# One unit's input product moves from GpSimd to VectorE in two thirds of the jobs of a selective-scan layer

## The chip, the cores and the metric

The kernel runs on one core of a Trainium2 chip. The metric is device time in microseconds of that core, as the median of three timed runs. One further execution was taken with the hardware profiler; its page and its trace are what the document reads. The engines are named as the profile names them: PE (TensorE matmuls; PEld its weight loads), DVE (VectorE), ACT (ScalarE), POOL (GpSimd), SP (the queue that issues the DMAs).

## The reference

An image batch (8, 192, 56, 56) goes through four residual layers, each `x = x + layer(groupnorm(x))`. Layer 0 is an involution. Layers 1, 2 and 3 are selective state-space blocks (Mamba), and this change touches layer 1 alone. Cut to what matters there:

```
# layer 1: 192 channels are cut into 3 slices of 64, each slice is one sequence of 3136 tokens
xs = layernorm(x) cut into 3 slices
xz = xs @ in_proj_W.T                     # 512 channels xi, 512 channels z
xc = silu(causal conv of xi, 4 taps)
dbl = xc @ x_proj_W.T                     # 4 columns for dt, 16 for B, 16 for C
dt = softplus(dbl[:4] @ dt_proj_W.T + b)
h  = h * exp(dt * A) + (dt * xc) * B      # 512 channels x 16 states, step by step along the sequence
y  = sum over states of h * C + xc * D
out = (y * silu(z)) @ out_proj_W.T
```

## The kernel before

Layer 1 walks over 8 images x 7 chunks of 448 tokens x 3 slices: 168 jobs. The three slices of a chunk are three jobs in a row, in slot 0, 1 and 2 (`jobs[i][0]`); "second- and third-slot jobs" are those of slots 1 and 2. After a chunk's third job, the layer norm and the projection of that chunk run inside the next slot-0 job.

A job has 512 channels x 16 states. They are cut into 16 units m = 0..15: 4 groups j of 128 channels, and in each group 4 quarters q of 4 states. A unit's tile `uhg` has 128 partitions (32 channels x 4 states) and 4 rows of 448 tokens, in 9 rotating buffers. For every unit:

- **product** `uhg = rep * B`: (dt x) times B. For some units VectorE makes it (`inputs_by_vector`, L754), from B in the one PSUM bank `b`, which PE fills with a selection matmul (`spread_b`, L723). For the others GpSimd makes it (`inputs_by_pool`, L748), from B in rows that a DMA has spread in SBUF (`row_in`). Here `pool_units` holds the odd units: eight each.
- **decays** (`decays`, L729): ACT writes exp(dt A) to the PSUM tiles `da0` and `da1`, one for each half of the unit.
- **scan** (L758): VectorE, two instructions, one for each half, on `uhg` in place; it needs `da` and the product.
- **keep** (L762): ACT copies the last column for the next chunk; `inputs_begin` (L737) copies it into the first column of a later unit's tile.
- **readout** (L767): GpSimd multiplies by C in place.
- **reduce** (L776): PE adds over the states into the bank `y`, behind a first matmul with D (L773). `gated` (L792): VectorE multiplies a finished group into the gate `zs`.

The order on each engine is that in which the loop over units issues (the scheduler is manual). In unit k it is: row DMAs, gated, reduce(k-3), planned steps, scan(k, first half), decays(k+1, first half), product of unit k+2 on GpSimd if it is one of its units, readout(k-2), product of unit k+1 on VectorE, `spread_b(k+2)`, planned steps, scan(k, second half), keep(k), decays(k+1, second half).

The planned steps are the next job's projections, put into 32 places (two for each unit) by `places`, with the stretches of `bounds`. For layer 1 the silu block has the places 6 and 7, that is unit 3. There ACT loads another function table (L596), makes silu on `xc` of the next job (1792 columns) and on the gates `zs` of the running job (L577), and loads the first table again (L569). Beside it, behind `spread_b` in unit 3, PE has the output projection of the job before (`out_proj`, L1054 and L1056), whose result ACT copies in unit 4 (L1061). In unit 4 PE has `xproj` (L601) and then `spread_b` for unit 6. Softplus has units 7 and 8 for a next job in slot 1, and units 9 and 10 otherwise.

`nothing` (L782) issues matmuls with zeros, so that PE has work in places where little is planned. Layers 2 and 3 have three channel groups (`nd == 3`), 12 units a job and another set of GpSimd units.

Of the kernel before, what the change touches and what calls it, by code (L numbers as in the profile page):

```python
# [86 lines left out]
def conv_mamba_stack(ctx: ExitStack, tc: tile.TileContext, a, out):  # L87
# [483 lines left out]
    def with_gates(ops, u):  # L571


        def all_ops():
            ops()
            if u is not None:
                nc.scalar.activation(u.zs, u.zs, AF.Silu)  # L577

        table_block(all_ops)
# [112 lines left out]
    def ssm_layer(pool, w, jobs, n_slots):  # L692


        nd = w.nd
        units = [(i, j, q) for i in range(len(jobs)) for j in range(nd) for q in range(NQ)]
        groups = [(i, j) for i in range(len(jobs)) for j in range(nd)]
        per_job = nd * NQ
        pool_units = {1, 3, 5, 7, 9, 11, 13, 15} if nd == 4 else {1, 3, 6, 7, 9, 11}
        pool_rows = sorted({m % NQ for m in pool_units})  # L700
        us = [Layer() for _ in jobs]
        carry = []
        for s in range(n_slots):
# [13 lines left out]
        def spread_b(k):  # L717

            if k in by_pool:
                return  # L720
            i, j, q = units[k]
            brow[k] = banks.b.tile([128, 512], F32, tag="b", name="b")
            nc.tensor.matmul(brow[k][:, :T], lhsT=pick_b[:, q, :], rhs=us[i].parts, start=True, stop=True)  # L723

        def decays(k, h):
            i, j, q = units[k]
            t = banks.da[h]
            for r in range(2):
                nc.scalar.activation(  # L729
                    t[:, 64 + 449 * r : 512 + 449 * r], reps[k // NQ][:, 2 * h + r, 0, :], AF.Exp, scale=w.neg_a[:, j * NR + 2 * h + r, q : q + 1]  # L730
                )

        def inputs_begin(k):
            i, j, q = units[k]
            uhg[k] = pool.tile([128, NR, T + 1], F32, tag="uhg", name="uhg", bufs=9)
            before = zeros[:, :NR] if jobs[i][1] else carry[jobs[i][0]][:, j, q, :]
            nc.scalar.copy(uhg[k][:, :, 0:1], before.unsqueeze(2))  # L737

        by_pool = {k for k in range(len(units)) if (k % per_job) in pool_units}

        def inputs_by_pool(k):
            if k not in by_pool:
                return
            i, j, q = units[k]
            b = us[i].rows[0, q].unsqueeze(1).to_broadcast([128, NR, T])
            nc.gpsimd.tensor_mul(uhg[k][:, :, 1:], reps[k // NQ][:, :, 1, :], b)  # L748

        def inputs_by_vector(k):  # L750
            if k in by_pool:
                return
            b = brow[k][:, :T].unsqueeze(1).to_broadcast([128, NR, T])
            nc.vector.tensor_mul(uhg[k][:, :, 1:], reps[k // NQ][:, :, 1, :], b)  # L754

        def scan(k, h):
            v = uhg[k][:, 2 * h : 2 * h + 2, :].rearrange("p r t -> p (r t)")
            nc.vector.tensor_tensor_scan(v, banks.da[h][:, 63:961], v, 0.0, ALU.mult, ALU.add)  # L758

        def keep(k):  # L760
            i, j, q = units[k]
            nc.scalar.copy(carry[jobs[i][0]][:, j, q, :].unsqueeze(2), uhg[k][:, :, T:])  # L762

        def readout(k):
            i, j, q = units[k]
            v = uhg[k][:, :, 1:]
            nc.gpsimd.tensor_mul(v, v, us[i].rows[1, q].unsqueeze(1).to_broadcast([128, NR, T]))  # L767

        def reduce(k):
            i, j, q = units[k]  # L770
            if q == 0:
                ys[k // NQ] = banks.y.tile([128, 512], F32, tag="y", name="y")
                nc.tensor.matmul(ys[k // NQ][:, :T], lhsT=w.dd[:, j, :], rhs=us[i].xc[:, j, :], start=True, stop=False)  # L773
            y = ys[k // NQ]
            for r in range(NR):
                nc.tensor.matmul(y[32 * r : 32 * r + 32, :T], lhsT=fold, rhs=uhg[k][:, r, 1:], start=False, stop=(q == NQ - 1))  # L776

        def nothing(k, n):

            if k >= 0 and units[k][2] < NQ - 1:  # L780
                for _ in range(n):
                    nc.tensor.matmul(  # L782
                        ys[k // NQ][:, : nd * 112], lhsT=zeros, rhs=w.dd.rearrange("p j e -> p (j e)")[:, : nd * 112],
                        start=False, stop=False,
                    )

        def load_of(steps):
            return sum(st.cost for st in steps if st.matmuls)

        def gated(g):  # L790
            i, j = groups[g]
            nc.vector.tensor_mul(us[i].zs[:, j, :], us[i].zs[:, j, :], ys[g][:, :T])  # L792

        n_places = 2 * per_job
        def bounds(job):

            silu = 8 if nd == 3 else 6
            softplus = silu + (6 if nd == 3 else 8 if job[0] == 1 else 12)
            return (0, silu), (silu, silu + 2), (silu + 2, softplus), (softplus, softplus + 1), (softplus + 2, softplus + 4), (softplus + 4, n_places)

        def places(*stretches):

            plan = [[] for _ in range(n_places)]
            for steps, first, end in stretches:
                todo, debt = list(steps), 0.0
                for p in range(first, end):
                    room, closed = (sum(st.cost for st in todo) + debt) / (end - p) - debt, False
                    while todo and (room > 1e-6 and not closed or p == end - 1):  # L810
                        if (todo[0].block if p % 2 else todo[0].settles) and p < end - 1:
                            break
                        plan[p].append(todo[0])
                        closed = todo[0].closes
                        room -= todo.pop(0).cost
                    debt = max(0.0, -room)
            return plan
# [12 lines left out]
        for k in range(3):  # L830
            inputs_begin(k)
        inputs_by_vector(0)
        spread_b(1)
        inputs_by_pool(0)
# [6 lines left out]
        def load_when_free(k):  # L841

            g = len(reps)
            if g < len(groups) and k >= NQ * g - NQ - 1 and groups[g][1] in us[groups[g][0]].ops:
                load_ops(g)

        for k, (i, j, q) in enumerate(units):
            m = k % per_job
            if m == 0:

                fetch, outs, rest = tail
                if i + 1 < len(jobs):
                    u = us[i + 1]
                    at = bounds(jobs[i + 1])
                    stretches = *jobs[i + 1][2](u, us[i], outs), rest + jobs[i + 1][3](u)
                    plan = places(*((steps, *p) for steps, p in zip(stretches, at)))
                else:
                    gates = Step(None, lambda: with_gates(lambda: None, us[i]), 0, 0.3, block=True)
                    plan = places(([gates], 4, 6), (outs + rest, 8, n_places))
                plan[3][:0] = [Step(None, fetch, 2, 0.0)]  # L860

            if i + 1 < len(jobs) and m - (per_job - NQ) in pool_rows:
                us[i + 1].row_in(0, m - (per_job - NQ))
            if i and m < NQ:
                us[i].row_in(1, m)
            if k >= NQ + 3 and q == 3:
                gated(k // NQ - 1)
            if k >= 3:
                reduce(k - 3)

            more = 3 - math.ceil(load_of(plan[2 * m] + plan[2 * m + 1]))
            nothing(k - 3, more > 2)
            bg.run(plan[2 * m])
            nothing(k - 3, more > 0)
            load_when_free(k)
            scan(k, 0)
            if k + 1 < n_units:
                decays(k + 1, 0)
            if k + 3 < n_units:
                inputs_begin(k + 3)  # L880
            if k + 2 < n_units:
                inputs_by_pool(k + 2)
            if k >= 2:
                readout(k - 2)
            if k + 1 < n_units:
                inputs_by_vector(k + 1)
            if k + 2 < n_units:
                spread_b(k + 2)
            bg.run(plan[2 * m + 1])
            nothing(k - 3, more > 1)  # L890
            load_when_free(k)
            scan(k, 1)
            keep(k)
            if k + 1 < n_units:
                decays(k + 1, 1)
            if m == per_job - 1:
                tail = jobs[i][4](us[i])
# [333 lines left out]
```

## Time and profile before

| | |
|---|---|
| median of the runs | 25021.5 us (25021.35 to 25040.56) |
| the profiled execution | 25031.88 us, its span 25030.1 us |
| layer 1, first scan of its first job to that of layer 2 | 1683 to 17177 us, 15494 us |
| busy share of the span | PE 85%, DVE 90%, ACT 68%, POOL 93% |
| POOL busy in the three jobs from 7170.86 to 7445.08 us | 270.06 of 274.22 us |
| DVE busy in the same stretch | 251.96 us |
| one product on POOL (L748) and on DVE (L754) | 3990 ns, 1997 ns |
| one half scan (L758), one readout (L767) | 2008 ns, 3678 ns |
| mean granted TensorE clock | 0.82 |

How to read it: a row of groups gives the line in the kernel, the engine, the operation, what is written from what, the shape, how often, then the busy time in us and the mean of one in ns, then the idle time of the engine just before it and what ended that. PEclk is the TensorE clock that was granted, as a share of full speed; in this trace it is either whole or half at any moment, and it changes on a fixed grid of 3.41 us.

### The profile page before, as it was taken

To read this page: it belongs to the slowest core of one execution; us is meant where nothing else is said; L and a number is where in the kernel's file an instruction comes from. 1 tells how busy PE (TensorE), PEld (TensorE's weight loads), DVE (VectorE), ACT (ScalarE), POOL (GpSimd) and SP (SyncE) were. 2 spreads that over 40 slices of the span, in tenths; PEclk is the share of its full clock that TensorE was granted. 3 is DMA by queue.
4 is the path that set the end of the run, shared out by engine and by line. 5 is a ranking of instruction groups with operands and counts; after the bars stand their busy time and mean duration, and the time that the engine had idled before them with its cause. 6 is when DMAs were issued, how large, how long until landed. Compare 5 with 4: busy or idle time off the path is not lost.

```text
span 25030.1 us, 232222 instructions
## 1 busy us (share of the span) xinstructions
PE 21294.5 (85%) x71980; PEld 6723.5 (27%) x71980; DVE 22624.9 (90%) x15661; ACT 16939.4 (68%) x32354; POOL 23378.2 (93%) x6772
## 2 busy tenths in 40 slices
PE   9988888888888888888888888888888887888888
PEld 3322222222222222222222222222333332333332
DVE  8879999999999999999999999997999998999998
ACT  1137777777777777777777777776777776777777
POOL 4459999999999999999999999998999998999999
PEclk9987777777777777777777777778888888888888
DMA  4433333333333333333333333333434443444443
GB/s 108 102 103 125 121 120 125 123 122 121 126 122 122 123 123 121 124 121 122 125 123 121 124 120 123 126 121 112 137 132 137 139 139 123 138 140 143 139 143 127
DMA packets 1184873, 3132.62 MB, mean 125 GB/s; under 512 B 163756, under 2 KB 446404, under 8 KB 1183496
## 3 DMA queue, kind: packets, MB, share of 16 engines
q1 hardware_dynamic: 1180824, 3116.70, 37.9%
q8 instruction: 565, 9.26, 0.1%
q14 instruction: 684, 5.60, 0.1%
q10 hardware_dynamic: 2800, 1.06, 0.0%
HBM read 2399.92 MB, written 555.55 MB: 118 GB/s over the span
## 4 chain that ended last, share of the span: by engine, by line
DVE 33%; PE 27%; ACT 17%; issue 11%; POOL 6%; DMA 5%; SPq 1%; DVEq 0%; POOLq 0%; ACTq 0%
DVE uhg L758 24%; ACT da L729 8%; DVE uhg L754 6%; PE y L776 4%; PE mm L635 4%; POOL uhg L767 4%; PE mm L416 3%; DMA rows<-bc 2%; PE y L782 2%; POOL uhg L748 2%; ACT L569 2%; PE y L773 2%; DMA rep<-ops 2%; PE y_inv L451 2%; PE mm L612 2%
## 5 line engine op out<-in xcount | busy, mean ns | idle before, releaser
L758 DVE TENSOR_TENSOR_SCAN uhg<-da,uhg 128x898 f32<-128x898 f32 x8064 | 15905.2, 2008 | 1283.9 <-ACT da L729 1272.0
L767 POOL TENSOR_TENSOR uhg<-uhg,rows 128x1792 f32<-128x1792 f32 x4032 | 14744.6, 3678 | 262.0 <-ACT carry L762 254.5
L729 ACT ACTIVATE da<-rep,k 128x448 f32<-128x448 f32 x16128 | 10253.6, 636 | 1659.5 <-DVE uhg L758 1280.4
L748 POOL TENSOR_TENSOR uhg<-rep,rows 128x1792 f32<-128x1792 f32 x2016 | 8043.7, 3990 | 489.8 <-DMA rows<-bc 235.6
L776 PE MATMUL y<-uhg,k 128*32 128x448 f32 x32256 | 4799.6, 671 | 738.5 <-POOL uhg L767 736.5
L754 DVE TENSOR_TENSOR uhg<-rep,b 128x1792 f32<-128x1792 f32 x2016 | 4025.6, 1997 | 444.5 <-PE b L723 399.9
L762 ACT COPY carry<-uhg 128x4 f32<-128x4 f32 x4032 | 787.3, 195 | 3545.3 <-DVE uhg L758 3452.2
L773 PE MATMUL y<-xc,w_d 128*128 128x448 f32 x2016 | 1505.0, 841 | 1437.3 <-DVE zs L792 1435.8
L782 PE MATMUL y<-w_d,k 128*128 128x448 f32 (+1 forms) x5276 | 2492.0, 580 | 0.0
L776 PEld LDWEIGHTS y<-uhg,k 128*32 128x32 f32 x32256 | 696.5, 117 | 3845.4 <-issue 2186.1
L635 PE MATMUL mm<-dbl,w_dt 36*128 36x448 f32 (+1 forms) x2016 | 1488.5, 851 | 150.1 <-ACT k L617 150.1
L1082 PE MATMUL mm<-v,w_in 96*128 96x448 f32 x2688 | 1460.9, 676 | 160.4 <-ACT zs L674 69.6
L782 PEld LDWEIGHTS y<-w_d,k 128*128 128x128 f32 x5276 | 1048.0, 213 | 1473.8 <-issue 1446.2
L1026 PE MATMUL mm<-xs,k 128*128 128x448 f32 x2688 | 1211.5, 585 | 120.6 <-ACT zs L674 108.7
L436 POOL TENSOR_TENSOR x<-x,one 96x448 f32<-96x448 f32 x560 | 633.3, 1135 | 669.1 <-DVE one L428 651.5
L428 DVE TENSOR_TENSOR prod<-mm,shifted 128x448 f32<-128x448 f32 x1680 | 932.4, 609 | 207.9 <-PE mm L416 187.5
L1109 PE MATMUL mm<-xin,w_conv 128*128 128x448 f32 x2688 | 1076.4, 543 | 1.9 <-ACT xin L674 1.0
L612 PE MATMUL mm<-dbl,k 16*16 16x448 f32 x1120 | 684.3, 699 | 424.7 <-ACT dbl L605 424.7
L773 PEld LDWEIGHTS y<-xc,w_d 128*128 128x128 f32 x2016 | 450.2, 262 | 2098.0 <-DVE zs L792 1419.4
L647 PE MATMUL mm<-xc,k 128*128 128x448 f32 x2016 | 972.2, 593 | 32.8 <-DVE dt L650 31.7
L1044 PE MATMUL mm<-xs,k 64*128 64x448 f32 x1344 | 860.6, 749 | 98.3 <-ACT zs L674 98.3
L723 PE MATMUL b<-k,k 96*128 96x448 bf16 x2016 | 826.5, 410 | 129.7 <-DVE uhg L754 129.5
(134 smaller groups left out, 19622.5 us busy)
## 6 DMA issues: line engine op xcount, KB each, us to landing
rep<-ops SPq DMA_DIRECT2D x4032, 448.0 KB, 5.8
ops<-dt SPq DMA_DIRECT2D x1008, 448.0 KB, 3.2
rows<-bc SPq DMA_DIRECT2D x1792, 224.0 KB, 6.2
shifted<-xpad SPq DMA_DIRECT2D x672, 179.0 KB, 4.6
xg<-stream SPq DMA_DIRECT2D x168, 336.0 KB, 3.9
xr<-stream SPq DMA_DIRECT2D x168, 336.0 KB, 5.2
stream<-xr SPq DMA_DIRECT2D x112, 336.0 KB, 3.3
xs<-xg SPq DMA_DIRECT2D x224, 112.0 KB, 2.3
```

The lines of the kernel that those rows point to most:

```text
L612: nc.tensor.matmul(u.left[m][:NS, :T], lhsT=ident[:NS, :NS], rhs=u.dbl[:NS, :], start=True, stop=False)
L635: nc.tensor.matmul(u.dps[j][:, :T], lhsT=w.dtw[:, j * 128 : (j + 1) * 128], rhs=u.dbl[:nk, :], start=True, stop=True)
L729: nc.scalar.activation(t[:, 64 + 449 * r : 512 + 449 * r], reps[k // NQ][:, 2 * h + r, 0, :], AF.Exp, scale=w.neg_a[:, j * NR + 2 * h + r, ...
L748: nc.gpsimd.tensor_mul(uhg[k][:, :, 1:], reps[k // NQ][:, :, 1, :], b)
L754: nc.vector.tensor_mul(uhg[k][:, :, 1:], reps[k // NQ][:, :, 1, :], b)
L758: nc.vector.tensor_tensor_scan(v, banks.da[h][:, 63:961], v, 0.0, ALU.mult, ALU.add)
L767: nc.gpsimd.tensor_mul(v, v, us[i].rows[1, q].unsqueeze(1).to_broadcast([128, NR, T]))
L773: nc.tensor.matmul(ys[k // NQ][:, :T], lhsT=w.dd[:, j, :], rhs=us[i].xc[:, j, :], start=True, stop=False)
L776: nc.tensor.matmul(y[32 * r : 32 * r + 32, :T], lhsT=fold, rhs=uhg[k][:, r, 1:], start=False, stop=(q == NQ - 1))
L782: nc.tensor.matmul(ys[k // NQ][:, : nd * 112], lhsT=zeros, rhs=w.dd.rearrange("p j e -> p (j e)")[:, : nd * 112], start=False, stop=False,)
L1026: nc.tensor.matmul(pm[:, :T], lhsT=w.inconv[:, k, j * 128 : (j + 1) * 128], rhs=ck.xs[:, i, 2 - 2 * k : 2 - 2 * k + T], start=(k == 0), st ...
L1082: nc.tensor.matmul(pm[:, :T], lhsT=w.inw[:, k, m * 128 : (m + 1) * 128], rhs=ck.v[:, k, :], start=(k == 0), stop=(k == NCT - 1),)
```

## The change

In layer 1, in jobs of slot 1 and 2 (the last job of the layer excepted), unit 5 is taken out of the set of GpSimd. Its product is then VectorE's, and it isn't issued where VectorE's products stand (in the middle of the unit before): it is issued at the end of unit 3, behind the second half scan. `at[1][0]` is 6 for layer 1, so `at[1][0] // 2` is 3. `multiplied` keeps the product from being issued twice. `spread_b(5)`, which did nothing while unit 5 was GpSimd's, now puts a matmul into PE's queue in unit 3. That is 111 jobs: 111 POOL instructions less, 111 DVE instructions and 111 matmuls (each with a weight load) more. The rows of B that GpSimd reads are still loaded (`pool_rows` names the same quarters). For layers 2 and 3 the expression gives unit 6, which is GpSimd's, so nothing changes there.

```
-        pool_units = {1, 3, 5, 7, 9, 11, 13, 15} if nd == 4 else {1, 3, 6, 7, 9, 11}
-        pool_rows = sorted({m % NQ for m in pool_units})
+        def pool_units(i):
+            if nd == 3:
+                return {1, 3, 6, 7, 9, 11}
+            return {1, 3, 5, 7, 9, 11, 13, 15} - ({5} if jobs[i][0] and i + 1 < len(jobs) else set())
+        pool_rows = (1, 2, 3) if nd == 3 else (1, 3)
...
-        by_pool = {k for k in range(len(units)) if (k % per_job) in pool_units}
+        by_pool = {i * per_job + m for i in range(len(jobs)) for m in pool_units(i)}
+        multiplied = set()
...
         def inputs_by_vector(k):
-            if k in by_pool:
+            if k in by_pool or k in multiplied:
                 return
+            multiplied.add(k)
             b = brow[k][:, :T].unsqueeze(1).to_broadcast([128, NR, T])
             nc.vector.tensor_mul(uhg[k][:, :, 1:], reps[k // NQ][:, :, 1, :], b)
...
             scan(k, 1)
+            if i + 1 < len(jobs) and m == at[1][0] // 2 and k + 2 not in by_pool:
+                inputs_by_vector(k + 2)
             keep(k)
```

## The prediction

> **What bounds the kernel now.** First the page: busy time, the chain, the groups.
>
> ```profile
> PE 21294.5 (85%) x71980; PEld 6723.5 (27%) x71980; DVE 22624.9 (90%) x15661; ACT 16939.4 (68%) x32354; POOL 23378.2 (93%) x6772
> ...
> DVE 33%; PE 27%; ACT 17%; issue 11%; POOL 6%; DMA 5%; SPq 1%; DVEq 0%; POOLq 0%; ACTq 0%
> ...
> L748 POOL TENSOR_TENSOR uhg<-rep,rows 128x1792 f32<-128x1792 f32 x2016 | 8043.7, 3990 | 489.8 <-DMA rows<-bc 235.6
> ...
> L754 DVE TENSOR_TENSOR uhg<-rep,b 128x1792 f32<-128x1792 f32 x2016 | 4025.6, 1997 | 444.5 <-PE b L723 399.9
> ```
>
> POOL is the busiest engine and is 6% of the chain that ended last; DVE, PE and ACT are 77% of it. So the second view is who waited for whom, cut to layer 1 (1683 to 17177 us):
>
> ```profile
> DVE uhg L758 <- ACT da L729: 731.9, 407, 3.8
> ...
> DVE uhg L754 <- PE b L723: 341.1, 221, 2.7
> ...
> POOL uhg L767 <- ACT carry L762: 199.7, 171, 4.0
> ...
> PE y L776 <- POOL uhg L767: 169.9, 143, 3.8
> ```
>
> DVE waits for ACT's decays (the two table blocks of a job) and for PE's spread of B. POOL waits 171 times for a unit that isn't scanned yet. Those waits lie in units 10 to 14 of slot 1 and at the end of slot 0: there POOL has caught up with VectorE, once in every three jobs, so it carries no debt along. A test of this in the trace: in slot-0 jobs without an image's end, the readout of unit 0 starts 5.2 to 6.7 us behind its scan, by chance of the job, and the job takes 94.15 to 94.22 us whatever that lag is. Only one with 7.3 us is longer, 94.44. So POOL, 98% busy in layer 1, runs behind a pace that VectorE, ACT and PE set.
>
> Third, the timeline of one slot-1 job around its unit 3, PE's and VectorE's rows:
>
> ```profile
> 7279.11 1.02 PE L773 MATMUL y<-xc,w_d 128*128 128x448 f32 x2 [3.10 <-DVE zs L792]
> 7280.06 1.70 PE L776 MATMUL y<-uhg,k 128*32 128x448 f32 x8
> 7281.69 1.75 PE L1054 MATMUL mm<-xs,k 64*64 64x448 f32 x2
> 7283.37 4.99 PE L1056 MATMUL mm<-zs,w_out 128*64 128x448 f32 x8
> 7288.29 0.96 PE L776 MATMUL y<-uhg,k 128*32 128x448 f32 x8
> 7289.18 3.20 PE L601 MATMUL mm<-xc,w_x 128*36 128x448 f32 x8
> 7292.31 0.36 PE L723 MATMUL b<-k,k 96*128 96x448 bf16 x1
> ...
> 7280.92 1.99 DVE L754 TENSOR_TENSOR uhg<-rep,b 128x1792 f32<-128x1792 f32 x1
> 7282.83 2.01 DVE L758 TENSOR_TENSOR_SCAN uhg<-da,uhg 128x898 f32<-128x898 f32 x1
> 7287.69 5.87 DVE L758 TENSOR_TENSOR_SCAN uhg<-da,uhg 128x898 f32<-128x898 f32 x3 [2.85 <-ACT da L729]
> 7293.47 2.00 DVE L754 TENSOR_TENSOR uhg<-rep,b 128x1792 f32<-128x1792 f32 x1
> ```
>
> VectorE's hole of 2.85 us is the silu block. The last DVE row is unit 6's product; its L723 ended at 7292.67, 0.80 us before. PE has no hole from 7279.11 on, and runs at half clock in 7280.1 to 7287.0 (the stretches in which PE's clock is half are in the trace; here two steps of its 3.41 us grid), since it stood still for 3.10 us before. The same place in a job that kept the full clock:
>
> ```profile
> 7100.26 3.22 PE L1056 MATMUL mm<-zs,w_out 128*64 128x448 f32 x8
> ...
> 7107.43 0.36 PE L723 MATMUL b<-k,k 96*128 96x448 bf16 x1
> ```
>
> Its L723 ends at 7107.79, 4.1 us before unit 6's product. Read in this way, 67 of 108 jobs of slots 1 and 2 have 0.8 us there, 7 have 2.5, 34 about 4.
>
> Last, the grid. Units 8 and 9 run up to and hold the softplus in slots 1 and 2. They take 13.74, 14.85 and 11.56 us in three jobs with the same instructions, by where the half-clock stretches fall:
>
> ```profile
> 7125.86:7139.60 13.74, 13.74 (x45) 4.39 (x43) 10.87 (x9) 12.02 (x21) 13.74 (x4) 0.73 0.15 58
> 7307.46:7322.31 14.85, 14.85 (x44) 4.83 (x42) 10.87 (x9) 12.03 (x21) 14.85 (x5) 0.66 0.15 60
> 7588.54:7600.10 11.56, 11.56 (x43) 4.17 (x43) 10.95 (x8) 11.10 (x19) 11.56 (x4) 0.85 0.19 74
> ```
>
> (The first column is the stretch, the third from the right the granted clock.) Three jobs in a row take 275.33 and 274.22 us in turn, together 549.55, which is 161 steps of 3.4133 us: the loop has locked to the clock's grid.
>
> **The change part by part.**
>
> POOL loses 111 products of 3.99 us, 443 us. I take 0 of it as gain: its cover isn't needed, POOL waits already. Ends: 0, and 443 us if every one of those waits were POOL's debt in disguise (a rival). What it does: POOL's lag falls by up to 4 us in slots 1 and 2 and in the slot 0 behind them; in slot 1 it becomes waiting for scans.
>
> VectorE gains 111 products of 1.997 us, 222 us. Each starts behind the second half scan of unit 3 (7284.84) and ends at about 7286.8; the decays come at 7287.65. The silu block on ACT (table load, two silus, table load, 7280.46 to 7286.33 in its timeline) hides it with 0.85 us to spare, so 0. If B were late, that spare would go first. What it needs is B in the bank: L723 for unit 5 must follow unit 4's product (one bank, ends 7282.91), 0.06 us for the semaphore and 0.37 at half clock, so it is ready at 7283.4, 1.4 us early. Behind the new product on VectorE's queue stands only the scan of unit 4. ACT's keep and decays wait for the scan before it. Buffers are free: unit 5's tile is the one that POOL would have written some 10 us before.
>
> PE gains 111 matmuls of 0.36 us, and here is the cost, by order and not by length: L723 for unit 5 stands in PE's queue behind the reduce and ahead of L1054, and it waits for VectorE. L1054 started at 7281.69; now it starts at 7283.4, 1.7 us later. PE idles 1.2 us, and the whole queue (L1054, L1056, reduce, L601, L723 of unit 6) moves. How far depends on the clock:
>
> - The half clock ends at the same step of the grid, 7287.0. Then fewer of the eight L1056 rows (0.75 us each at half, 0.375 at full) are slow: the end of L1056 moves by 0.9 to 1.05 us, L723 of unit 6 by as much; 0.80 us of that is spare, so VectorE loses 0.1 to 0.3 us.
> - It lasts one step more, 3.41 us. All of L1054 and L1056 is slow, 7.7 us: they end at 7291.1 where 7288.3 was, L1061 on ACT and the decays of unit 5 come 1.3 us late, L723 of unit 6 2.6 us: VectorE loses 1.8 us.
>
> Which: in the trace, half clock ends behind a step in which matmuls with 96 or 128 contraction rows filled 0.65 to 0.73 or more; those with 16, 36 or 64 (L1054) hardly count. With the new wait L1056 fills 0.55 of the second step in slot 1 (the step ends 8.0 us behind the unit's first scan) and 0.66 in slot 2 (8.3 us). So I take 1.8 us for the 46 jobs of slot 1 with 0.8 us to spare and 0.3 for the 21 of slot 2: 83 + 6 = 89 us. Ends: 67 x 0.1 = 7 us, and 67 x 1.8 = 121 us. In the 41 others the shift of 2 to 3.5 us (a full-clock job may now fall to half, since PE's 1.9 us hole is added to the 3.10) stays inside 2.5 to 4.1 us of spare: 0, at most 34 x 1.8 = 61 us.
>
> Grid: a loss moves all later work against the grid. Ends by the rows above: 11.56 and 14.85 us for units 8 and 9. Most slot-1 jobs stand at 14.85 now, and half of slot 2 at 13.74. If all 111 went to 11.56: 55 x 3.3 + 27 x 3.3 + 27 x 2.2 = about -330 us; if slot 2 all went to 14.85: +30 us. I take 0, since a lock holds its place until another is as near: two turns of three jobs at 161 steps (549.55) become 162 (552.96) when some 3.4 us are added, 1.7 for each turn, 55 x 1.7 = 94 us, close to the 89.
>
> Sum: 0 + 0 + 89 + 0. The profiled execution's 25031.9 is 10.4 above the median of 25021.5; on the median it makes 25110.
>
> A rule weighed: the Trainium skill, "Perfetto Trace Analysis", section Identifying the Most-Contended Engine, says that the engine with the highest occupancy is the most contended and is to be improved first. By it GpSimd's 443 us come off, 24578 us; this trace's waits speak against it, by them the sum is 25110.
>
> **The rivals.**
>
> 1. *POOL sets the pace after all* (faster, 24578 to 24850). For it: 98% busy, and PE waits 170 us for readouts in layer 1. Against: the chain, the constant slot-0 time. Price 443 us at most; 170 us if only PE's waits are bought.
> 2. *The grid turns kind* (faster). Where units 8 and 9 fall to 11.56 us in half of the 111 jobs, -165 us, against up to 89 of loss: about 24930. It decides once the new shift carries the half-clock stretch off these units in more than some 30 jobs. For it: jobs at an image's end have it. Against: the lock returns to the old place within one turn after each image.
> 3. *The lateness stays in the spare* (same). The half clock ends in time in both slots: 7 to 30 us, 25040.
>
> **How the numbers follow.** A difference under 0.2% (50 us) counts as same, about what a measurement of this kernel can tell. Forecast 0.50 (slower, 25110); rival 3 0.25 (same); rival 2 0.18 and rival 1 0.07 (both faster). The slower case alone reaches from 25075 to 25210 (121 + 61 us). The range, with rival 2 in and half of its better side: 24920 to 25220.
>
> **What would show it.** In the profile after: L748's successor on POOL has 111 rows less, and POOL waits more for ACT's carry. Unit 5's product lies in VectorE's hole, which shrinks from 2.85 to 0.85 us. L1054's successor starts 1.7 us later, and the waits of VectorE's products for `b` grow (341 us now) by about what the kernel loses. Wrong if POOL shows no more idle time and the kernel is faster by hundreds of us; or if the three-job turn is shorter with L1056 late all the same, which would be the grid.

## The result, and the profile after

The changed kernel took 25308.8 us (median of 4 executions, 25285.5 to 25318.2); the kernel before took 25026.7 us beside it (25021.4 to 25040.6). The ratio is 1.0115, with a 95% interval of 1.0103 to 1.0127: 282 us slower. The profiled execution is one of the four, at 25318.18 us, its span 25316.2 us. Lines that belong together have moved by the diff: L748, L754, L758, L767, L723, L729, L1056, L1061 of before are L755, L762, L766, L775, L729, L735, L1066, L1071 of after.

The page of after: busy time, the chain that ended last by engine, and the groups that answer to those shown of before.

```profile
PE 21389.1 (84%) x72091; PEld 6765.7 (27%) x72091; DVE 22871.8 (90%) x15772; ACT 16920.2 (67%) x32354; POOL 22968.5 (91%) x6661
...
DVE 30%; PE 30%; POOL 12%; ACT 12%; issue 10%; DMA 5%; SPq 1%; DVEq 0%; POOLq 0%; ACTq 0%
...
L775 POOL TENSOR_TENSOR uhg<-uhg,rows 128x1792 f32<-128x1792 f32 x4032 | 14754.3, 3674 | 972.8 <-ACT carry L770 962.0
...
L755 POOL TENSOR_TENSOR uhg<-rep,rows 128x1792 f32<-128x1792 f32 x1905 | 7591.8, 3985 | 496.7 <-DMA rows<-bc 263.1
...
L762 DVE TENSOR_TENSOR uhg<-rep,b 128x1792 f32<-128x1792 f32 x2127 | 4251.9, 1999 | 558.5 <-PE b L729 513.6
```

The change did what it says: 111 products left POOL (2016 to 1905), 111 came to VectorE (2016 to 2127). POOL is busy 410 us less. Its share of the chain rose from 6% to 12% all the same; it is 12% as well in the kernel below that has the new matmul alone and leaves POOL all its work, so this share does not price POOL's relief.

Who waited for whom, in layer 1 of after (1658 to 17460 us; us in total, times, longest):

```profile
POOL uhg L775 <- ACT carry L770: 908.2, 773, 3.8
...
DVE uhg L766 <- ACT da L735: 612.2, 492, 3.4
DVE uhg L762 <- PE b L729: 458.9, 383, 2.0
...
ACT y L1071 <- PE mm L1066: 202.6, 106, 15.1
```

POOL waits 773 times for a unit that isn't scanned yet, 171 times before. VectorE's wait for B rose by 118 us (341.1 before). Its wait for decays fell by 120 us only, though the new product fills 1.91 us of the silu hole in each of 111 jobs, which is 212 us: 92 us of new waits for decays must have come in. The last line says where from: ACT's copy of the output projection's result, L1071, waits 106 times for PE, where L1061 of before waited twice.

One slot-1 job of after around its unit 3, PE's rows and then VectorE's (start, length, line, how many; in brackets the idle time before the row and what ended it):

```profile
7366.85 1.02 PE L781 MATMUL y<-xc,w_d 128*128 128x448 f32 x2 [3.11 <-DVE zs L800]
7367.80 1.54 PE L784 MATMUL y<-uhg,k 128*32 128x448 f32 x8
7370.70 0.53 PE L729 MATMUL b<-k,k 96*128 96x448 bf16 x1 [1.36 <-DVE uhg L762]
7371.16 1.75 PE L1064 MATMUL mm<-xs,k 64*64 64x448 f32 x2
7372.84 5.90 PE L1066 MATMUL mm<-zs,w_out 128*64 128x448 f32 x8
...
7382.69 0.36 PE L729 MATMUL b<-k,k 96*128 96x448 bf16 x1
```

```profile
7368.65 1.99 DVE L762 TENSOR_TENSOR uhg<-rep,b 128x1792 f32<-128x1792 f32 x1
...
7372.50 1.99 DVE L762 TENSOR_TENSOR uhg<-rep,b 128x1792 f32<-128x1792 f32 x1
7375.42 3.94 DVE L766 TENSOR_TENSOR_SCAN uhg<-da,uhg 128x898 f32<-128x898 f32 x2 [0.93 <-ACT da L735]
7380.55 2.03 DVE L766 TENSOR_TENSOR_SCAN uhg<-da,uhg 128x898 f32<-128x898 f32 x1 [1.18 <-ACT da L735]
7383.09 2.02 DVE L762 TENSOR_TENSOR uhg<-rep,b 128x1792 f32<-128x1792 f32 x1 [0.52 <-PE b L729]
```

The new matmul, L729 at 7370.70, waits for unit 4's product, which ends at 7370.64, and PE stands still for 1.36 us. The output projection behind it runs at half clock nearly to its end (5.90 us, 4.99 before) and is done at 7378.74. ACT's copy and the decays behind it come late, so VectorE waits 1.18 us before unit 5's scan; then L729 of unit 6 comes late, and it waits another 0.52 us. The new product itself, at 7372.50, costs nothing: the hole ahead of unit 4 was 2.85 us and is 0.93.

Measured from unit 4's first scan to unit 6's, these two units took 9.63 us in 110 of 111 jobs of before. In after they take 11.54 us in 46 of the 56 slot-1 jobs, 11.3 to 11.4 in four, 9.63 in six, and 11.20 us in all 55 slot-2 jobs. That is 95 + 86 = 181 us.

The rest lies in the turn of three jobs. Here are two turns of before and one of after (stretch, its length, then busy time and number of PE, PEld, DVE, ACT, POOL, then the granted clock, the DMA share and GB/s):

```profile
6895.53:7170.86 275.33, 233.43 (x727) 66.96 (x725) 251.98 (x153) 195.99 (x375) 268.17 (x73) 0.77 0.36 123
7170.86:7445.08 274.22, 229.70 (x707) 66.34 (x708) 251.96 (x153) 195.78 (x373) 270.06 (x75) 0.78 0.36 123
```

```profile
7258.55:7538.44 279.89, 232.44 (x718) 67.04 (x718) 256.43 (x155) 195.36 (x373) 261.89 (x73) 0.77 0.36 120
```

Away from an image's end, a turn of after is 279.89 us, one like the other, which is 82.0 steps of the 3.4133 us clock grid; before it was 80.34 and 80.66 steps by turns. Over the layer, the first turn left out, a turn's mean grew from 274.91 to 280.46 us, 5.6 us. Units 4 and 5 of slots 1 and 2 are 3.3 of them. The other 2.3 us lie for the most part where the instructions did not change and the half-clock stretches did: unit 1 of slot 2 (6.07 to 7.62 us on average), unit 11 of slot 1 (8.53 to 9.46), with unit 1 of slot 1 shorter (6.30 to 5.78). Layer 1 grew by 308 us, 15494 to 15802. That is 26 us more than the medians differ, since layer 0, which is the same in both, was 25 us shorter in this profiled execution.

### The profile page after: what moved, and what is told of

It is laid out like the page before. It is cut to its first block, busy times and chain, and to the rows that moved or that the text cites. A ratio compares the mean times of both kernels' runs of the same rounds, so it can differ in the third digit from the quotient of the medians.

```text
span 25316.2 us, 232229 instructions
## 1 busy us (share of the span) xinstructions
PE 21389.1 (84%) x72091; PEld 6765.7 (27%) x72091; DVE 22871.8 (90%) x15772; ACT 16920.2 (67%) x32354; POOL 22968.5 (91%) x6661
## 4 chain that ended last, share of the span: by engine, by line
DVE 30%; PE 30%; POOL 12%; ACT 12%; issue 10%; DMA 5%; SPq 1%; DVEq 0%; POOLq 0%; ACTq 0%
DVE uhg L766 20%; POOL uhg L775 8%; DVE uhg L762 7%; ACT da L735 5%; PE y L784 5%; POOL uhg L755 5%; PE mm L635 3%; DMA rows<-bc 3%; PE mm L416 3%; PE y L790 3%; PE mm L1066 2%; PE y L781 2%; PE y_inv L451 2%; DMA rep<-ops 2%; PE mm L612 1%
## 5 line engine op out<-in xcount | busy, mean ns | idle before, releaser
L766 DVE TENSOR_TENSOR_SCAN uhg<-da,uhg 128x898 f32<-128x898 f32 x8064 | 15918.8, 2009 | 1167.3 <-ACT da L735 1153.0
L775 POOL TENSOR_TENSOR uhg<-uhg,rows 128x1792 f32<-128x1792 f32 x4032 | 14754.3, 3674 | 972.8 <-ACT carry L770 962.0
L735 ACT ACTIVATE da<-rep,k 128x448 f32<-128x448 f32 x16128 | 10252.9, 636 | 1675.1 <-DVE uhg L766 1298.4
L755 POOL TENSOR_TENSOR uhg<-rep,rows 128x1792 f32<-128x1792 f32 x1905 | 7591.8, 3985 | 496.7 <-DMA rows<-bc 263.1
L762 DVE TENSOR_TENSOR uhg<-rep,b 128x1792 f32<-128x1792 f32 x2127 | 4251.9, 1999 | 558.5 <-PE b L729 513.6
L635 PE MATMUL mm<-dbl,w_dt 36*128 36x448 f32 (+1 forms) x2016 | 1432.7, 821 | 336.4 <-ACT k L617 336.4
L729 PE MATMUL b<-k,k 96*128 96x448 bf16 x2127 | 828.4, 389 | 421.0 <-DVE uhg L762 420.9
L1054 PE MATMUL mm<-xs,k 64*128 64x448 f32 x1344 | 856.4, 743 | 53.9 <-ACT zs L674 53.9
L1092 PEld LDWEIGHTS mm<-v,w_in 96*128 96x128 f32 x2688 | 582.0, 233 | 1069.5 <-issue 444.1
```

The lines of the kernel that those rows point to most:

```text
L635: nc.tensor.matmul(u.dps[j][:, :T], lhsT=w.dtw[:, j * 128 : (j + 1) * 128], rhs=u.dbl[:nk, :], start=True, stop=True)
L735: nc.scalar.activation(t[:, 64 + 449 * r : 512 + 449 * r], reps[k // NQ][:, 2 * h + r, 0, :], AF.Exp, scale=w.neg_a[:, j * NR + 2 * h + r, ...
L1092: nc.tensor.matmul(pm[:, :T], lhsT=w.inw[:, k, m * 128 : (m + 1) * 128], rhs=ck.v[:, k, :], start=(k == 0), stop=(k == NCT - 1),)
```

## The experiments

Two theories stood at the start. The first is the prediction's: one matmul in PE's queue, which waits for VectorE ahead of the output projection, costs it all. The rivals: VectorE's 222 us of added products cost something after all; or the relief of POOL moves the loop against the clock's grid.

### One part of the change at a time

**The matmul alone.** Before, with a matmul into bank `b` whose result nobody reads, at the place where the change puts it. POOL still makes the product.

```
             if k + 2 < n_units:
                 spread_b(k + 2)
+            if nd == 4 and m == 3 and jobs[i][0] and i + 1 < len(jobs):
+                unread = banks.b.tile([128, 512], F32, tag="b", name="b")
+                nc.tensor.matmul(unread[:, :T], lhsT=pick_b[:, 1, :], rhs=us[i].parts, start=True, stop=True)
```

> The kernel before, with one thing of the change: in unit 3 of the same 111 jobs PE gets a matmul that writes B of unit 5 into the one bank b, behind unit 4's product and ahead of the output projection; nobody reads it, and GpSimd still makes unit 5's product. Theory 1 (the wait in PE's queue is the cost): all of the loss is here, units 4 and 5 together take 11.2 to 11.6 us in slots 1 and 2 where they took 9.63, and the time is 200 to 320 us above before. Theory 2 (the cost is VectorE's extra product, or the moved work, and not PE's order): within 50 us of before.

Measured: 25303.4 us (25281.5 to 25323.1), ratio 1.0109 [1.0094, 1.0124], against 25036.1 us of the kernel before beside it. PE's and VectorE's rows of a slot-1 job (its L891 is the added matmul, L1059 the output projection):

```profile
7372.05 0.53 PE L891 MATMUL b<-k,k 96*128 96x448 bf16 x1 [1.34 <-DVE uhg L754]
7372.51 1.75 PE L1057 MATMUL mm<-xs,k 64*64 64x448 f32 x2
7374.19 5.89 PE L1059 MATMUL mm<-zs,w_out 128*64 128x448 f32 x8
```

```profile
7376.78 3.95 DVE L758 TENSOR_TENSOR_SCAN uhg<-da,uhg 128x898 f32<-128x898 f32 x2 [2.84 <-ACT da L729]
7381.95 2.03 DVE L758 TENSOR_TENSOR_SCAN uhg<-da,uhg 128x898 f32<-128x898 f32 x1 [1.23 <-ACT da L729]
7384.43 2.02 DVE L754 TENSOR_TENSOR uhg<-rep,b 128x1792 f32<-128x1792 f32 x1 [0.45 <-PE b L723]
```

The hole of PE, the late output projection, both new waits of VectorE and the turn of 82.0 steps are those of after, while the hole of 2.84 us stays open and POOL has all its work. So 111 matmuls of about half a microsecond make the whole loss, as far as the intervals tell (267 us here, 282 in after), and it needs neither the product nor POOL's relief.

**The product alone.** Before, with unit 4's product made a second time at the end of unit 3, from a B that is there already. No matmul is added and POOL keeps its work.

```
             scan(k, 1)
+            if nd == 4 and m == 3 and jobs[i][0] and i + 1 < len(jobs):
+                inputs_by_vector(k + 1)
             keep(k)
```

> The kernel before, with VectorE's part alone: at the end of unit 3 of the same 111 jobs VectorE makes unit 4's product a second time (same operands, same result, 2.0 us), in the place where the changed kernel makes unit 5's. GpSimd and PE keep their work. Theory 1: the silu block hides it, VectorE's hole before unit 4 shrinks from 2.84 to about 0.9 us and the time stays within 50 us. Theory 2: 111 x 2.0 = 222 us above before, or a good part of that.

Measured: 25023.7 us (24996.5 to 25040.1), ratio 0.9995 [0.9986, 1.0005]. VectorE's row:

```profile
7262.97 5.87 DVE L758 TENSOR_TENSOR_SCAN uhg<-da,uhg 128x898 f32<-128x898 f32 x3 [0.93 <-ACT da L729]
```

222 us of work on the second busiest engine cost nothing, as it lies in a wait; turns are 80.34 and 80.66 steps as before.

**POOL's relief alone.** Before, with the readout of unit 1 cut to 8 of 448 columns in the same 111 jobs; the multiplication by C is left out for the other columns. It takes about as much off POOL as the change does (its busy time falls by 356 us against before's profile).

```
-            v = uhg[k][:, :, 1:]
-            nc.gpsimd.tensor_mul(v, v, us[i].rows[1, q].unsqueeze(1).to_broadcast([128, NR, T]))
+            n = 8 if nd == 4 and k % per_job == 1 and jobs[i][0] and i + 1 < len(jobs) else T
+            v = uhg[k][:, :, 1 : n + 1]
+            nc.gpsimd.tensor_mul(v, v, us[i].rows[1, q][:, :n].unsqueeze(1).to_broadcast([128, NR, n]))
```

> The kernel before, with GpSimd's relief alone: in the same 111 jobs the readout of unit 1, which GpSimd starts in unit 3 where the changed kernel has one product less, multiplies 8 columns of each row and not 448 (the other columns go on without C, so this part of the computation is left out). GpSimd loses about 3.6 us in each of these jobs. Theory 1 (GpSimd has time to spare): within 50 us of before, GpSimd waits more for ACT's carry. The rival that GpSimd sets the pace: 111 x 3.6 = 400 us below before.

Measured: 25113.0 us (25106.7 to 25121.0), ratio 1.0034 [1.0021, 1.0047]. Less work on the busiest engine made the kernel slower, and the turns are 81.0 steps. A turn is 1.5 us longer on average, and 0.9 of it lies in unit 6 of slot 0. PE's rows of slot 0, first of before, then of this kernel, from 21.5 and 20.0 us behind the job's first scan on (before starts this turn at 7170.86, this kernel at 7200.83):

```profile
7192.33 0.96 PE L776 MATMUL y<-uhg,k 128*32 128x448 f32 x8 [1.42 <-POOL uhg L767]
7193.22 3.20 PE L601 MATMUL mm<-xc,w_x 128*36 128x448 f32 x8
...
7199.42 0.92 PE L612 MATMUL mm<-dbl,k 16*16 16x448 f32 x2 [1.83 <-ACT dbl L605]
...
7203.49 1.67 PE L612 MATMUL mm<-dbl,k 16*16 16x448 f32 x2
```

```profile
7220.81 0.96 PE L777 MATMUL y<-uhg,k 128*32 128x448 f32 x8
7221.69 3.20 PE L601 MATMUL mm<-xc,w_x 128*36 128x448 f32 x8
...
7229.40 1.67 PE L612 MATMUL mm<-dbl,k 16*16 16x448 f32 x2 [3.32 <-ACT dbl L605]
...
7234.65 1.67 PE L612 MATMUL mm<-dbl,k 16*16 16x448 f32 x2
```

In before PE waits 1.42 us for a readout of POOL and does the next projection (L601) 1.5 us later. L612 starts at the same time in both, 28.56 and 28.57 us behind the job's start, because it waits for ACT. So without POOL's delay PE's hole ahead of L612 grows from 1.83 to 3.32 us (3.3 in 46 of 54 slot-0 jobs; the median of before is 1.9). In the step of the clock's grid from 7224.80 to 7228.22 PE is then busy for only 0.37 of the time (0.82 in the step of before that answers to it), and the clock is half behind it: half clock begins at 27.4 us of the job, where it was 30.8, the second L612 comes 1.2 us later against the job's start, and unit 6 takes 5.78 us instead of 4.35 to 4.85. POOL's lateness had been spreading PE's work over the grid.

Another 0.9 us of the turn lies in unit 1 of slot 1 (6.30 to 7.21 us on average: 7.6 us or more in 39 of 54 jobs, in 15 before), ahead of the place of the edit, and unit 9 of slot 2 gave 0.4 back.

**Half of the change: slot 1 only.**

```
-            return {1, 3, 5, 7, 9, 11, 13, 15} - ({5} if jobs[i][0] and i + 1 < len(jobs) else set())
+            return {1, 3, 5, 7, 9, 11, 13, 15} - ({5} if jobs[i][0] == 1 and i + 1 < len(jobs) else set())
```

> The change in slot 1 alone (55 or 56 of the 111 jobs). A plain sum of delays: half of the loss, about 140 us, 25160 to 25180. Theory of the grid: units 4 and 5 of slot 1 take 1.7 to 1.9 us more, and the turn then goes to the next lock, 81 or 81.5 steps (25110 to 25210) or stays at 82 (25310); slot 2 has 9.63 us there.

Measured: 25102.7 us (25077.9 to 25119.9), ratio 1.0033 [1.0021, 1.0045]; turns of 81.0 steps. Its PE rows in a slot-1 job, then VectorE's:

```profile
7316.13 0.53 PE L729 MATMUL b<-k,k 96*128 96x448 bf16 x1 [1.58 <-DVE uhg L762]
7316.59 1.75 PE L1064 MATMUL mm<-xs,k 64*64 64x448 f32 x2
7318.27 4.32 PE L1066 MATMUL mm<-zs,w_out 128*64 128x448 f32 x8
```

```profile
7326.94 2.02 DVE L762 TENSOR_TENSOR uhg<-rep,b 128x1792 f32<-128x1792 f32 x1 [0.22 <-PE b L729]
```

The same edit in the same slot costs 0.3 us in 40 of the 56 jobs here, where 1.7 to 1.9 were expected (nothing in eleven, 1.8 to 1.9 in five), and 1.9 in after. Here the half clock ends 8.4 us behind unit 3's first scan, early enough for part of L1066; in after it lasts to 11.6 us. What the edit costs is set by where the job stands on the grid, and slot 2's share of the change moves where slot 1 stands. The other 60 us or so of this kernel's loss lie in unit 1 of slot 1 above all (6.30 to 6.99 us on average) and in no step of the edit.

In after itself, slot 2 shows how the clock is lost. The granted clock is the third figure from the right; the stretches are steps of the grid:

```profile
7460.24:7463.65 3.41, 1.79 (x11) 0.39 (x3) 3.41 (x4) 3.13 (x8) 2.86 (x2) 1.00 0.00 0
7463.65:7467.07 3.42, 1.48 (x11) 0.29 (x10) 3.42 (x3) 3.39 (x3) 3.42 (x2) 0.99 0.44 143
7467.07:7470.48 3.41, 3.41 (x6) 0.98 (x6) 3.41 (x2) 3.38 (x4) 3.41 (x1) 0.50 0.91 290
7470.48:7473.89 3.41, 3.41 (x5) 0.94 (x5) 2.48 (x3) 2.33 (x6) 2.39 (x2) 0.51 0.28 110
```

```profile
7466.76 0.35 PE L729 MATMUL b<-k,k 96*128 96x448 bf16 x1 [1.94 <-DVE uhg L762]
7467.03 1.75 PE L1064 MATMUL mm<-xs,k 64*64 64x448 f32 x2
7468.72 5.75 PE L1066 MATMUL mm<-zs,w_out 128*64 128x448 f32 x8
```

The new wait is 1.94 us long, and no longer one lies in that step; with it PE is busy for 1.48 of the step's 3.42 us, and the clock is half in the next. That step is full, but half of it is L1064 with 64 contraction rows, and the clock stays half for another. So in slot 2 the new hole does not lengthen a half-clock stretch, it makes one.

The Trainium skill, "TensorE: Matmul & The Clock Gate", section Part 1: The HAM clock gate, gives a free-running window of 4096 cycles, 3413 ns, over which activity is judged; the 3.4133 us grid of these traces agrees. Its section Why this matters for your kernels asks for no idle gap above some 3 us between bursts. Here the measurement says more: a gap of 1.94 us was enough, with PE busy for 43% of the step.

### Taking the wait away

**Another bank for unit 5's B.** After, with B of unit 5 in a bank of the rotating `mm` pool. Its matmul then does not wait for unit 4's product; the product of unit 5 and POOL's relief stay.

```
-            brow[k] = banks.b.tile([128, 512], F32, tag="b", name="b")
+            early = nd == 4 and k % per_job == 5
+            brow[k] = mm_tile() if early else banks.b.tile([128, 512], F32, tag="b", name="b")
```

> The changed kernel, but B of unit 5 goes into a bank of the projections' pair (mm), which is free by then, so PE does not wait for unit 4's product; order and number of instructions are the changed kernel's. Theory 1: the output projection starts 0.4 us later than before and not 1.7 us, units 4 and 5 take 9.6 to 9.8 us again, and the time comes back to within 80 us of before (25020 to 25100), the rest being where the clock's grid locks. Theory 2: as slow as the changed kernel, 25280 to 25320.

Measured: 25100.2 us (25085.0 to 25115.9), ratio 1.0029 [1.0018, 1.004]. PE's rows of a slot-1 job, where L730 is the matmul and L1067 the output projection:

```profile
7296.55 0.36 PE L730 MATMUL mm<-k,k 96*128 96x448 bf16 x1
7296.85 0.96 PE L1065 MATMUL mm<-xs,k 64*64 64x448 f32 x2
7297.74 3.22 PE L1067 MATMUL mm<-zs,w_out 128*64 128x448 f32 x8
...
7302.50 3.17 PE L601 MATMUL mm<-xc,w_x 128*36 128x448 f32 x8 [0.66 <-DVE uhg L763]
```

No hole ahead of L730, full clock, and units 4 and 5 are back to 9.63 us in all jobs. The wait has not gone altogether: L601 in unit 4 now waits for unit 5's product, which reads B from a bank of the pair (0.66 us here; 93 times and 61.0 us in layer 1), but behind the output projection, where it costs these units nothing. What is left is 64 us by the medians, at turns of 81.0 steps, with slot 0's unit 6 at 5.78 us in 45 of 54 jobs and slot 1's unit 1 at 7.21 on average: the same picture as with POOL's relief alone.

**Work ahead of the wait.** After, with one matmul of zeros ahead of the waiting one in the same 111 places.

```
+            if nd == 4 and m == 3 and jobs[i][0] and i + 1 < len(jobs):
+                nothing(k - 3, 1)
             if k + 2 < n_units:
                 spread_b(k + 2)
```

> The changed kernel with one matmul of zeros (two passes, 0.75 us at full clock, 1.5 at half) in unit 3 of the 111 jobs, between the reduce and the matmul that waits for VectorE: it fills PE's new hole with work that the clock counts, and moves nothing later, since PE stands there anyway. Theory 1 with the clock (the wait costs mostly because PE stays at half clock for the output projection behind it): half clock ends one 3.41 us step earlier, units 4 and 5 of slots 1 and 2 fall from 11.2 to 11.5 us to 9.6 to 10.3, and the time falls by 150 to 300 us, to 25020 to 25160. Without the clock (only the order costs): 25280 to 25320 stays.

Measured: 25106.5 us (25080.6 to 25119.8), ratio 1.0031 [1.0019, 1.0044].

```profile
7313.94 1.02 PE L790 MATMUL y<-w_d,k 128*128 128x448 f32 x2
7315.95 0.35 PE L729 MATMUL b<-k,k 96*128 96x448 bf16 x1 [0.99 <-DVE uhg L762]
7316.23 0.96 PE L1066 MATMUL mm<-xs,k 64*64 64x448 f32 x2
7317.12 3.22 PE L1068 MATMUL mm<-zs,w_out 128*64 128x448 f32 x8
```

The wait is still there, 0.99 us of idle time and 1.0 of zeros, but the output projection runs at full clock and VectorE loses nothing in units 4 and 5 (9.63 us in 109 of 111 jobs). So the wait costs through the clock. What stays is again 81.0 steps and slot 0's unit 6 at 5.78 us.

### Is the remainder POOL's relief?

In the two kernels above and in the one with POOL's relief alone PE runs dry in slot 0: its hole ahead of L612 is 3.3 us in 46 or 47 of 54 jobs. If that is the cause, zeros in slot 0's unit 4 should end it.

```
             nothing(k - 3, more > 0)
+            nothing(k - 3, 3 if nd == 4 and m == 4 and not jobs[i][0] else 0)
```

> The changed kernel with the matmul of zeros ahead of the waiting one (25107 us by itself) and three more in unit 4 of slot 0 alone. It tells whether the rest of the loss, 80 us, is GpSimd's relief that lets PE run dry in slot 0: if so, unit 6 of slot 0 falls from 5.78 to 4.35 to 4.85 us and the time to that of before or below, 24940 to 25050; if not, 25100.

Measured, on top of the zeros ahead of the wait: 25016.4 us (24977.0 to 25043.8), ratio 0.9998 [0.9988, 1.0007]. Turns are 80.34 and 80.66 steps again, the hole ahead of L612 is 1.0 us or less, slot 0's unit 6 takes 4.35 to 4.85 us and slot 1's unit 1 6.62 on average (7.25 without these zeros). The whole loss of the change is gone, within the interval, with the change in place, and nothing was done but to give PE zeros to multiply: one in unit 3 of slots 1 and 2, three in unit 4 of slot 0.

The control, two zeros in slot 0's unit 4 of the kernel before:

```
+            nothing(k - 3, 2 if nd == 4 and m == 4 and not jobs[i][0] else 0)
```

> The kernel before with two matmuls of zeros in unit 4 of slot 0, where its hole is 1.6 to 2.9 us. If filling that hole is worth something by itself, the kernel before gains too (25 to 100 us); if slot 0 of the kernel before already keeps the clock, within 50 us.

Measured: 24994.9 us (24976.1 to 25033.4), ratio 0.999 [0.9981, 1.0000]: at most a small gain where POOL still delays PE. So of the 90 us that the zeros in slot 0 brought above, some 30 by the medians, and at most 48 by the interval, might have come without POOL's relief too.

### Zeros in other places

Four kernels with zeros in unit 5 or in unit 4, or spread over slot 0. The first two have two zeros in unit 5 of every job:

```
+            if nd == 4 and m == 5:
+                nothing(k - 3, 2)
```

On the kernel before:

> The kernel before with two more matmuls of zeros in unit 5 of every job of layer 1, where PE waits 1 to 3 us for ACT's copy of the next job's projection. Theory of the grid (the turn of three jobs takes a whole or half number of 3.41 us steps, and which one is set by where PE stands still): half clock begins later or not at all in units 5 to 7, the turn locks elsewhere, 78 to 80 steps or 81 to 82: the time moves by 50 us or more, and the turn is again a whole or half number of steps. If PE's clock did not matter to the pace: within 30 us of before, with the turn at 274.8 us.

Measured: 25163.1 us (25139.7 to 25169.4), ratio 1.0055 [1.004, 1.007]. Unit 6 of slot 0 grew from 4.65 to 7.02 us on average: in unit 5 the zeros stand ahead of work for softplus (L635), and delay it: in one such job they take 3.35 us at half clock, and ACT waits 2.69 us for the projection behind them. Turns are 81.45 and 81.67 steps with some of 79.6 to 80, so not every turn sits on a whole or half step.

On the kernel with the other bank:

> The changed kernel with B of unit 5 in the projections' bank (no wait on PE) and with the two matmuls of zeros in unit 5 of every job: both together. The other-bank kernel took 25100 us, at 81 steps a turn, because slot 0 fell to half clock a step earlier (unit 6 took 5.78 us and not 4.35 to 4.85). If zeros in unit 5 keep the clock there, 80 steps a turn or fewer, 24800 to 25000, below both kernels; if they only delay PE, 25100 or more.

Measured: 25272.3 us (25261.3 to 25288.3), ratio 1.0101 [1.0086, 1.0116]. The gain that was expected did not come. Unit 6 of slot 0 is 8.83 us on average, and turns settle at 82.0 steps.

In unit 4, where PE waits for ACT's copy in any case, on the kernel with the other bank:

```
+            nothing(k - 3, (2 if jobs[i][0] else 3) if nd == 4 and m == 4 else 0)
```

> The changed kernel with B of unit 5 in the projections' bank, and matmuls of zeros in unit 4, behind the projection xproj (three in slot 0, two in slots 1 and 2; 0.75 us each at full clock), ahead of unit 6's B, which has 4.1 and 3.1 us to spare there. They shorten PE's hole before the next matmuls of unit 5 (3.3 us in this kernel without them) by 1.5 to 2.3 us. Theory of the grid: half clock then begins a step later, unit 6 of slot 0 falls from 5.78 to 4.35 to 4.85 us, and the turn goes below 81 steps: 80 or 80.5, 24920 to 25040. If the hole is not what sets it: 25100 as without the zeros.

Measured: 24950.1 us (24939.4 to 24961.2), ratio 0.9969 [0.9958, 0.9981]; turns about 80.1 steps and 79.9 by turns, slot 0's unit 6 at 4.44 and unit 7 at 9.35 us (4.65 and 10.28 before).

In slot 0 alone, there also in units 13 and 15:

```
+            nothing(k - 3, (3 if m == 4 else m in (13, 15)) if nd == 4 and not jobs[i][0] else 0)
```

> The changed kernel with B of unit 5 in the projections' bank, zeros in slot 0 alone: three in unit 4, one each in units 13 and 15, to end the half clock that runs from unit 12 of slot 0 into unit 1 of slot 1 (where unit 1 takes 7.8 us and not 5.77). If it ends a step or more sooner, slot 1's unit 1 falls to 5.77 and the turn by one half to one step, 24900 to 25000; if PE is only held up, 25100 or more.

Measured: 24918.0 us (24905.5 to 24968.3), ratio 0.9961 [0.9946, 0.9976], faster than both kernels. One of its turns:

```profile
7120.95:7394.02 273.07, 226.67 (x728) 66.36 (x728) 255.79 (x155) 195.29 (x373) 261.58 (x73) 0.81 0.37 123
```

273.07 us is 80.0 steps, and it is so turn for turn away from an image's end. PE has more instructions than in after (728 to 718) and is busy 5.8 us less per turn, since the granted clock is 0.81 instead of 0.77. Units 6 and 7 of slot 0 are 4.35 and 8.74 us, units 8 and 9 of slot 1 4.42 and 7.43 (5.12 and 9.24 before); unit 1 of slot 1 gave some back, 8.46 against 6.30. How much of this the same zeros would give on the kernel before, with its own unit 5 on POOL, was not measured.

## Why the prediction was right or wrong

- **POOL does not set the pace: right.** 443 us of products left it, and none of it came back as time. "I take 0 of it as gain" held, and rival 1 is out. The rule that was weighed, of the Trainium skill, "Perfetto Trace Analysis", section Identifying the Most-Contended Engine, pointed at the busiest engine; less work on it alone measured 0.34% slower. But its ends, 0 to 443 us of gain, did not hold a loss. With PE's wait away, POOL's relief costs 64 to 89 us (the medians of the other bank, of the zeros ahead and of the cut readout against their own kernel before), by PE running dry in slot 0; zeros there took it back. That PE waits 170 us for readouts was read as a possible gain alone. In after that cost does not add to the matmul's: the matmul alone and the whole change are both at 82.0 steps and 1.09% and 1.15%, with overlapping intervals. There slot 0 meets the grid in another phase: half clock falls into unit 3 (13.9 to 17.3 us of the job in one turn), L601 starts at 22.4 us as in before without any wait for POOL, the hole ahead of L612 is 1.8 us in 52 of 54 jobs (53 with the matmul alone), and unit 6 takes 4.5 us.
- **VectorE's product in the silu hole: right.** The hole went to 0.93 us (0.85 forecast), and the product alone costs nothing.
- **One waiting matmul in PE's queue: the right mechanism.** The experiment with the matmul alone shows it to be the whole loss, by the path that was named: output projection, ACT's copy, decays, B of unit 6. L1064 starts 4.44 us behind the unit's first scan, 1.73 later than before (1.7 forecast), though the matmul takes 0.53 us at half clock and not 0.37. One sign was too simple: the waits for `b` grew by 118 us, not by what the kernel lost, since much of the loss comes as waits for decays.
- **Its size in slot 1: right for each job, too few jobs.** 1.8 us for 46 jobs was forecast; 46 jobs lost 1.9 us and four more 1.7 to 1.8, 95 us against 83.
- **Its size in slot 2: the first failed step.** "0.3 for the 21 of slot 2" and 0 for the rest there; all 55 jobs lost 1.57 us, 86 us against 6. The step took slot 2's half-clock stretch from before, lengthened or not. In after the stretch of before isn't there any more: the jobs reach unit 3 in another phase at full clock, and the new hole takes the clock away itself, for two steps, through L1064 and most of L1066. That "the 41 others" would keep their spare fell for the same reason. The case of 0.3 us exists: with the change in slot 1 alone it was measured, 0.30 us.
- **The rule for the clock: too coarse.** "[T]hose with 16, 36 or 64 (L1054) hardly count" holds for 16 and 36 rows, not for 64. In before, half clock ended behind 24 steps filled to 0.74 or 0.75 by matmuls with 128 rows and to about 0.28 by those with 64; it went on behind 67 steps filled to 0.77 or 0.78 by 128 rows and for the rest by 16 or 36. If each matmul's time is weighted by its contraction rows over 128, the steps of before and after in layer 1 sort better: behind those under 0.45 the full clock was always lost, behind those over 0.53 it was always kept; behind those under 0.83 half clock always went on, behind those over 0.85 it always ended.
- **The grid: the second failed step.** "I take 0, since a lock holds its place until another is as near", with two turns going from 161 to 162 steps. They went to 164. Beyond the 181 us of units 4 and 5 the turn took some 2.3 us more, about 127 us over the layer, and the bound for a loss there was 30 us. That bound was worked out for units 8 and 9 of slots 1 and 2; the time came in unit 1 of slot 2 and unit 11 of slot 1, which the step had not looked at.
- **The sum.** 89 us forecast, 282 us measured: 25308.8 us lies above the range of 24920 to 25220. In layer 1 of the profiled execution, which lost 308 us, the 89 lacked 92 us in units 4 and 5 and about 127 us of the grid.
- **Rivals 2 and 3** did not come. A kind grid exists, at 80.0 steps, but it took work for PE in the right places.

What stays open is why the turn settles at 82.0 steps and not at 81.5 for a direct loss of 3.3 us per turn. The places of the other 2.3 us are named above, but the runs do not derive them, and no experiment moved the phase alone.

## What to carry to other kernels

A matmul that waits in PE's queue is priced by what stands behind it and by the clock that the hole costs, not by its length: 111 of half a microsecond cost 1.1%. Before an instruction with a wait goes into an in-order queue, ask whether its buffer can come free earlier (with another bank a shorter wait was left at a later place, where it cost these units nothing) or whether independent work can stand ahead of it. And in a steady loop under a clock that is judged on a fixed grid, a job's phases of before can't be carried over to after: price the new hole in each place at any phase, or take the range from the worst one.

## What the runs showed that had not been expected

- Nearly every steady turn sat at one of a few lengths: 80.0, 80.34 and 80.66 by turns, 81.0, or 82.0 steps of 3.4133 us, in twelve of the fourteen kernels (with the other bank and zeros in unit 5, only four of an image's seven turns did). The two others are those with zeros in unit 4 of all slots (79.9 and 80.1 by turns, two turns 160 steps) and with zeros in unit 5 on before (81.45 and 81.67, some 79.6 to 80). Among the twelve an edit moved the mean turn by half a step or by one and a half, 1.7 or 5.1 us, or not at all.
- Taking some 3.2 us off the busiest engine (98% in this layer) in 111 jobs made the kernel 0.34% [0.21, 0.47] slower: its lateness had kept a hole of PE short (1.9 us, 3.3 without it).
- Matmuls of zeros in three units of slot 0 took the changed kernel with the other bank from a ratio of 1.0029 to 0.9961; two in unit 5 of every job took it to 1.0101.
